# A graph-convolution stage on one core: eight of 32 edge rows fetched by GpSimd's indirect DMAs instead of selected by one-hot matmuls

## The chip, the cores and the metric

The kernel runs on one NeuronCore of a Trainium2 chip. The metric is device time in microseconds of the whole program, from one launch; the lower the better. The engines are called PE (TensorE, the matmuls; PEld is its weight load), DVE (VectorE), ACT (ScalarE), POOL (GpSimd) and SP (SyncE, which here only issues DMAs).

## The reference

Two networks run on one graph of 12,500 nodes and 412,500 edges (400,000 drawn at random plus a loop at every node; `src` and `dst` are inputs and come sorted by `dst`). The first is a two-layer graph convolution with 16 features in, 32 hidden, 16 out:

```
deg  = segment_sum(ew with loops of weight 1, dst)
dis  = where(deg > 0, rsqrt(deg), 0);  norm = dis[src] * ew * dis[dst]
h    = relu(segment_sum((x  @ W1.T)[src] * norm, dst) + b1)
out  =      segment_sum((h  @ W2.T)[src] * norm, dst) + b2
x    = layernorm(x + out)        # over the 16 features
```

The second is a mesh network on the result: an edge encoder, a node encoder, and two rounds of edge MLP, segment sum over `dst` and node MLP, with a decoder. Its output is added to x, and a last layer norm over the features follows. The change concerns the graph convolution alone, and there the two lines with `segment_sum(... [src] ...)`: for each edge, a row of a table of 12,500 x 16 floats is taken by `src`, weighted, and added up by `dst`.

## The kernel before, in words

**Sorting.** The edges lie in 128 rows (one for each partition), each of 3,328 slots (`RL`), and each row spans a short stretch of destinations. A bitonic network on DVE sorts every row by source; the key is source times 128 plus the destination's offset from the row's base, and the edge weight moves along. The sorted keys are then taken apart: the source modulo 256 goes to DRAM as bf16 (`mod_d`), the source's block of 256 relative to a planned first block (`slot_t`), the destination's offset (`drel_t`) and the weight (`ew_t`) are turned by TensorE, so that 128 edges lie on the partitions. A row is then 26 tiles (`NS`) of 128 edges.

**Messages.** `messages(table, fill)` is called twice, once for each convolution. It fills the table, writes it to DRAM, and splits it into three bf16 parts that sum to the float (`parts3`, into `t3`, which stays in SBUF: 256 sources on two halves of 128 partitions, blocks of 256 along the free axis). A hardware loop of four trips then takes 32 rows (`RI`) a trip, with the loop's body written out. For each row:

- `load` (L577) has SP fetch the row's 3,328 values of `mod_d` broadcast to 128 partitions, 832 KB; this is issued one row ahead.
- `half_row` (L583) makes the one-hot over the source modulo 256, in bf16, two DVE operations of 128x1664 for each half of the row. `begin` (L589, L591) makes `wm`, which picks the block and carries the edge weight.
- `select` takes the row's 26 tiles in six packs, of 4, 4, 5, 5, 4 and 4 tiles. For each tile, six bf16 matmuls (L607: three parts by two halves of 128 sources) gather up to seven candidate blocks of 16 features per edge into PSUM. DVE makes the destination one-hot `ohd` (L611) and multiplies PSUM by `wm` into `msg` (L614).
- `add_up` (L623) multiplies `msg` by `ohd` on TensorE in fp32, one matmul for each tile (two instructions in the records), one pack behind `select`. After the last pack ACT copies the row's sum out of PSUM (L629).
- `fold_up` (L635, L639) adds the seven blocks with one matmul, and DVE adds the result to `agg` at the row's base.

The tile framework sets the order of each engine's instructions in this stage by its own planning; SP and POOL have queues of their own. POOL has nothing to do here. In the later edge stages it issues the indirect DMAs of `gather` (L415), each of which fetches 128 rows of 64 floats by 128 indices.

Names used below: L385 is the one-hot of the edge stage on DVE (two SBUF inputs, fp32, 128x512), L1116 another (one bf16 input), L405 the addition to a window, L1175 the edge update; L566 and L570 are the copies at the start of each trip of the message loop.

Of the kernel before, what the change touches and what calls it, by code (L numbers as in the profile page):

```python
# [9 lines left out]
F32 = mybir.dt.float32  # L10
I32 = mybir.dt.int32
BF16 = mybir.dt.bfloat16
# [19 lines left out]
RI = 32  # L32
EPS = 1e-5
# [4 lines left out]
def gcn_then_mesh_gnn_kernel(ctx: ExitStack, tc: tile.TileContext, a: dict, out: bass.AP):  # L38
# [86 lines left out]
    def bank(name):  # L125
        return psum.tile([128, 512], F32, name=f"ps_{name}")
# [80 lines left out]
    slot_t = so.tile([P, NS, NR], F32, name="slot_t")  # L207
    drel_t = so.tile([P, NS, NR], F32, name="drel_t")
    ew_t = so.tile([P, NS, NR], F32, name="ew_t")
    with tc.tile_pool(name="sort", bufs=1) as sp, \  # L210
# [94 lines left out]

        mod = sp.tile([NR, RL], BF16, name="mod")
# [35 lines left out]
        for t, to in ((free, slot_t), (k, drel_t), (vals[turn], ew_t)):  # L342
            for j0 in range(0, NS, 4):
                n = min(4, NS - j0)
                pt = pp.tile([128, 512], F32, name="ps_st", bufs=2)
                for j in range(n):
                    nc.tensor.transpose(pt[:, j * NR:(j + 1) * NR], tiles(t)[:, j0 + j, :], ident)
                nc.scalar.copy(to[:, j0:j0 + n, :], pt[:, :n * NR].rearrange("e (j r) -> e j r", r=NR))
# [156 lines left out]
    with tc.tile_pool(name="gcn", bufs=1) as gp, tc.tile_pool(name="gcnw", bufs=2) as gw:  # L505
# [10 lines left out]
        ior = gp.tile([P, LR], F32, name="ior")  # L516
        nc.gpsimd.iota(ior, pattern=[[1, LR]], base=0, channel_multiplier=0, allow_small_or_imprecise_dtypes=True)
# [34 lines left out]
        def messages(table, fill):  # L552
# [10 lines left out]
            with tc.tile_pool(name="rows", bufs=2) as rw:  # L563
                with tc.For_i(0, trip_count(2, NR // RI)) as it:
# [7 lines left out]
                    slot, drel, ew = mine  # L572
                    rows, loaded, sums, folds = {}, {}, [], []

                    def load(r):
                        loaded[r] = rw.tile([128, RL], BF16, name="mod")
                        nc.sync.dma_start(loaded[r], mod_d[ds(it * RI + r, 1), :].to_broadcast([128, RL]))  # L577

                    def half_row(r, h):

                        oh = rw.tile([128, 2, RL // 2], BF16, name="roh", bufs=3)
                        for i in range(2):
                            nc.vector.tensor_scalar(oh[:, i, :], loaded[r][:, h * (RL // 2):(h + 1) * (RL // 2)],  # L583
                                                    iof[:, i:i + 1], None, op0=OP.is_equal)
                        return oh

                    def begin(r):
                        wm = rw.tile([P, NS, SB], F32, name="wm")
                        nc.vector.tensor_tensor(wm, iow[:, None, :SB].to_broadcast([P, NS, SB]),  # L589
                                                slot[:, :, r:r + 1].to_broadcast([P, NS, SB]), op=OP.is_equal)  # L590
                        nc.vector.tensor_tensor(wm, wm, ew[:, :, r:r + 1].to_broadcast([P, NS, SB]), op=OP.mult)  # L591
                        ohs = [None, None]
                        h = packs[0][0] // (NS // 2)
                        ohs[h] = half_row(r, h)
                        rows[r] = ohs, wm, bank("seg")

                    def select(r, j0, n, sb):
                        ohs, wm, acc = rows[r]
                        pg = bank("h")
                        for j in range(j0, j0 + n):  # L600
                            h, at = divmod(j, NS // 2)
                            if ohs[h] is None:
                                ohs[h] = half_row(r, h)
                            b = first_block[r, j] * F
                            for i in range(3):
                                for u in range(2):
                                    nc.tensor.matmul(pg[:, (j - j0) * sb * F:(j - j0 + 1) * sb * F],  # L607
                                                     ohs[h][:, u, at * P:(at + 1) * P], t3[:, i, u, b:b + sb * F],
                                                     start=(i == u == 0), stop=(i == 2 and u == 1))
                        ohd = rw.tile([P, 5, LR], F32, name="ohd", bufs=3)  # L610
                        nc.vector.tensor_tensor(ohd[:, :n, :], ior[:, None, :].to_broadcast([P, n, LR]),  # L611
                                                drel[:, j0:j0 + n, r:r + 1].to_broadcast([P, n, LR]), op=OP.is_equal)
# [28 lines left out]
                    load(0)  # L641
                    for r in range(RI):
                        if r + 1 < RI:
                            load(r + 1)
                        begin(r)
                        for i, pack in enumerate(packs):
                            sums.append(select(r, *pack))
                            if len(sums) > 1:
                                add_up(*sums.pop(0))
                            if folds and i >= 2:  # L650
                                fold_up(*folds.pop(0))
                    add_up(*sums.pop(0))
                    fold_up(*folds.pop(0))
# [659 lines left out]
```

## Time and profile before

| | us |
|---|---|
| median of three runs | 15415.33 (15409.99 to 15437.33) |
| the profiled execution | 15403.32 |
| its span, first to last instruction | 15401.6 |
| busy PE / DVE / POOL / ACT over the span | 11359.6 / 8752.5 / 6386.7 / 2374.3 |

The profile records one execution; 1.7 us of it lie outside the span. In the order of time: the sort until about 800 us, the degrees until about 1300 us, the first message loop until about 3005 us, the second, after the layer between, from about 3130 to 4840 us, and the two edge stages up to the end. The message loops run at a clock of 0.99 of full speed, with PE busy 98% of the time, and POOL is idle in them. A row of the profile names the line, the engine, the operation, output and inputs, and shape; a bracket at its end tells how long the engine was idle before it and what released it.

### The profile page before, as it was taken

The page shows a single profiled execution, that of the slowest core. Times are in us where ns is not written, and L with a number is a line of the kernel's source. Part 1 is how long each engine was busy: PE and PEld are TensorE (multiplying, and loading weights), DVE is VectorE, ACT ScalarE, POOL GpSimd, SP SyncE. Part 2 cuts the span into 40 slices and gives each one's busy share as a digit, 9 for nine tenths or more (in the row PEclk, how much of TensorE's full clock was granted, in tenths as well). Part 3 has the DMA queues.
Part 4 walks back from the last instruction along what each step waited for, and adds up shares of the span by engine and source line. Part 5 has one row for each costly group of instructions (what it writes and reads, how often), then busy time and mean ns, then how long its engine had stood idle before and what let it go on. Part 6 is the DMA issues. An engine that isn't in the chain of part 4 may idle for free. (4 is left out here: it accounts for less than half of the span.)

```text
span 15401.6 us, 272960 instructions
## 1 busy us (share of the span) xinstructions
PE 11359.6 (74%) x104538; PEld 8563.0 (56%) x104539; DVE 8752.5 (57%) x22373; ACT 2374.3 (15%) x3731; POOL 6386.7 (41%) x6741
## 2 busy tenths in 40 slices
PE   0089999999998788888888888875666666666665
PEld 0078999889997455555555555553444444444443
DVE  9977777677777455455555555553444444444444
ACT  3400000000000222222222222221111111111111
POOL 0000000000001555556556665555666666666665
PEclk9999999999997688788888888886777777777777
DMA  0001111111111222222222222222222222222222
GB/s 29 0 15 54 66 64 66 50 67 66 65 65 47 56 59 59 58 60 62 59 59 62 59 62 60 60 60 59 61 60 60 61 60 60 61 60 60 61 59 50
DMA packets 958543, 871.49 MB, mean 57 GB/s; under 512 B 599416, under 2 KB 706192, under 8 KB 956548
## 3 DMA queue, kind: packets, MB, share of 16 engines
q1 hardware_dynamic: 258034, 493.54, 9.5%
q0 software_dynamic: 207360, 212.75, 6.8%
q10 hardware_dynamic: 491796, 147.08, 4.1%
q8 instruction: 859, 14.07, 0.4%
q14 instruction: 494, 4.05, 0.1%
HBM read 718.12 MB, written 134.51 MB: 55 GB/s over the span
## 5 line engine op out<-in xcount | busy, mean ns | idle before, releaser
L415 POOL DMA_INDIRECT pg<-tab_p,si x6480 | 6293.6, 971 | 3901.1 <-issue 1707.5
L1052 PE MATMUL ps_o<-eb_w,h 128*128 128x128 f32 x6480 | 1389.3, 381 | 1822.1 <-ACT h L1045 1623.5
L1052 PEld LDWEIGHTS ps_o<-eb_w,h 128*128 128x128 f32 x6480 | 1184.3, 274 | 2078.7 <-ACT h L1045 1762.4
L607 PE MATMUL ps_h<-t,roh 128*128 128x112 bf16 (+1 forms) x39936 | 2131.9, 211 | 65.9 <-DVE roh L583 65.9
L607 PEld LDWEIGHTS <-roh 128*128 128x128 bf16 x39936 | 2011.2, 98 | 115.3 <-issue 112.0
L789 POOL MEMSET zero<- 64x192 bf16 x1 | 0.3, 252 | 4015.1 <-DVE agg L639 4015.1
L1116 DVE TENSOR_SCALAR ot<-rb,iop 128x512 bf16<-128x512 bf16 x810 | 295.5, 365 | 2349.4 <-DMA rb<-relg_d 1482.8
L623 PE MATMUL ps_seg<-ohd,msg 128*112 128x112 f32 (+1 forms) x13312 | 1618.5, 266 | 0.0
L474 DVE TENSOR_REDUCE var<-sq 128x8 f32<-128x512 f32 (+2 forms) x1290 | 843.1, 666 | 1291.8 <-issue 743.9
L397 PE MATMUL ps_seg<-oh,y 128*64 128x64 f32 x19440 | 1298.7, 255 | 208.6 <-issue 197.9
L623 PEld LDWEIGHTS ps_seg<-ohd,msg 128*112 128x112 f32 (+1 forms) x13312 | 1407.4, 172 | 0.5
L397 PEld LDWEIGHTS ps_seg<-oh,y 128*64 128x64 f32 x19440 | 1141.8, 166 | 370.3 <-issue 348.0
L1040 PE MATMUL ps_h<-e,eb_w 128*128 128x512 f32 x1620 | 1193.3, 820 | 64.2 <-issue 36.4
L614 DVE TENSOR_TENSOR msg<-ps_h,wm 128x448 f32<-128x448 f32 (+1 forms) x1536 | 975.0, 635 | 460.5 <-PE ps_h L607 455.0
L611 DVE TENSOR_TENSOR ohd<-ior,rdrel 128x448 f32<-128x448 f32 (+1 forms) x1536 | 1011.1, 659 | 235.3 <-PE ps_seg L623 235.3
L473 ACT ACTIVATE sq<-ps_o 128x512 f32<-128x512 f32 (+1 forms) x1240 | 735.4, 593 | 2587.6 <-remote 668.8
L1045 ACT ACTIVATE h<-ps_h,eb_b 128x512 f32<-128x512 f32 x810 | 556.7, 687 | 3047.7 <-remote 2019.4
L1040 PE MATMUL ps_h<-ot,qd 128*128 128x512 bf16 x2430 | 784.4, 424 | 110.1 <-issue 97.3
L479 DVE TENSOR_TENSOR y<-ps_o,rs_y 128x512 f32<-128x512 f32 x1215 | 802.8, 688 | 88.1 <-issue 4.6
L385 DVE TENSOR_TENSOR oh<-iow,drl 128x512 f32<-128x512 f32 x1215 | 830.0, 683 | 14.4 <-DMA drl<-rel_d 7.2
L1042 PE MATMUL ps_h<-ident,pg 128*128 128x128 f32 x3240 | 603.1, 296 | 309.9 <-issue 236.5
L1052 PE MATMUL ps_o<-ee_w,h 128*128 128x128 f32 x3240 | 626.6, 353 | 238.5 <-ACT h L1033 232.8
(280 smaller groups left out, 11483.2 us busy)
## 6 DMA issues: line engine op xcount, KB each, us to landing
mod<-mod_d SPq DMA_DIRECT2D x256, 832.0 KB
pg<-tab_p,si POOLq DMA_INDIRECT x6480
e_d<-e SPq DMA_DIRECT2D x405, 256.0 KB
e<-e_d SPq DMA_DIRECT2D x405, 256.0 KB
rb<-relg_d ACTq DMA_DIRECT2D x1612, 64.0 KB
qd<-tab_q ACTq DMA_DIRECT2D x1612, 24.0 KB
at<-in_attrT SPq DMA_DIRECT2D x405, 32.0 KB
tab_q<-tabs SPq DMA_DIRECT2D x50, 187.5 KB
```

What stands on the lines that cost most here:

```text
L385: nc.vector.tensor_tensor(oh, iow[:, None, :].to_broadcast([P, K, W]), drl[:, g * K:(g + 1) * K, None].to_broadcast([P, K, W]), op=OP.is_e ...
L397: nc.tensor.matmul(ps[r:r + n, :W], v, oh[:, k, :], start=(k == 0), stop=(k == K - 1))
L415: nc.gpsimd.indirect_dma_start(out=to[:, k, :], out_offset=None, in_=table, in_offset=bass.IndirectOffsetOnAxis(ap=idx[:, k:k + 1], axis=0))
L473: nc.scalar.activation(sq, o.rearrange("p (k f) -> p k f", f=D), AF.Square, scale=D ** -0.5)
L474: nc.vector.tensor_reduce(v[:, i:i + k], sq, axis=AX.X, op=OP.add)
L479: nc.vector.tensor_tensor(y, o, r[:, i:i + k, None].to_broadcast(list(y.shape)), op=OP.mult)
L607: nc.tensor.matmul(pg[:, (j - j0) * sb * F:(j - j0 + 1) * sb * F], ohs[h][:, u, at * P:(at + 1) * P], t3[:, i, u, b:b + sb * F], start=(i ...
L611: nc.vector.tensor_tensor(ohd[:, :n, :], ior[:, None, :].to_broadcast([P, n, LR]), drel[:, j0:j0 + n, r:r + 1].to_broadcast([P, n, LR]), o ...
L614: nc.vector.tensor_tensor(msg[:, :n * sb * F].rearrange("p (j s f) -> p j s f", s=sb, f=F), pg[:, :n * sb * F].rearrange("p (j s f) -> p j ...
L623: nc.tensor.matmul(acc[:sb * F, :LR], msg[:, j * sb * F:(j + 1) * sb * F], ohd[:, j, :], start=(j0 + j == packs[0][0]), stop=((j0, n, sb) ...
L1040: nc.tensor.matmul(ph, w, v, start=(i == 0), stop=False)
L1052: nc.tensor.matmul(po[:, j * 128:(j + 1) * 128], h[:, j * P:(j + 1) * P], w1, start=False, stop=(j == KP - 1))
```

## The change

Eight of a trip's 32 rows (3, 6, ... 24) no longer go through `load`, `half_row`, `select`, `add_up` and `fold_up`. For them:

- After the sort, the full source numbers are also turned by TensorE, and the eight rows' part of each trip is kept as int32 (`src_t`). To make room, `slot_t` and `drel_t` become bf16.
- `fetch(i)` has POOL issue 26 indirect DMAs, each of which fetches 128 table rows of 16 floats from DRAM, into one of three buffers `xg`. Two fetches are issued at the start of a trip, and the others as earlier ones are begun.
- `gathered(i)` works on DVE and PE in ten pieces, one after each pack of the ordinary rows: multiply `xg` by the weight; split it into three bf16 parts (`parts3`, five operations); six times make a bf16 one-hot over 128 destinations for up to five tiles, with the 26 matmuls (one-hot as weights, 48 moving columns) one piece behind; copy the sum out on ACT; turn and add the three parts with three fp32 matmuls, and add to `agg`.
- `due` starts a gathered row with the ordinary rows number 4, 6, 9, 11, 13, 16, 18 and 20 of the 24.

The ordinary rows are begun one row ahead, their `begin` now in six steps, one after each pack (both halves' one-hots, and `wm`), and `load` is issued two rows ahead. `ohd` is issued ahead of the pack's matmuls rather than after them. PE, DVE and ACT are issued in the order of the source (`manual_schedule`), not in a planned one.

```diff
-    slot_t = so.tile([P, NS, NR], F32, name="slot_t")
-    drel_t = so.tile([P, NS, NR], F32, name="drel_t")
+    slot_t = so.tile([P, NS, NR], BF16, name="slot_t")
+    drel_t = so.tile([P, NS, NR], BF16, name="drel_t")
+    src_t = so.tile([P, NS, NR // RI * len(GR)], I32, name="src_t")
...
+        nc.vector.tensor_single_scalar(kj, ki, 7, op=OP.arith_shift_right)
+        nc.vector.tensor_copy(vals[1 - turn], kj)
+        srcf = sp.tile([P, NS, NR // RI, len(GR)], F32, name="srcf")
+        turned_tiles(vals[1 - turn], lambda j0, n, v: nc.scalar.copy(
+            srcf[:, j0:j0 + n], v.rearrange("e j (i r) -> e j i r", r=RI)[:, :, :, GR.start:GR.stop:GR.step]))
+        nc.vector.tensor_copy(src_t, srcf.rearrange("e j i r -> e j (i r)"))
...
                     def begin(r):
-                        wm = rw.tile([P, NS, SB], F32, name="wm")
...
+                        loaded_r = loaded.pop(r)
                         ohs = [None, None]
...
+                        first = packs[0][0] // (NS // 2)
+                        for h in (first, 1 - first):
+                            ohs[h] = rw.tile([128, 2, RL // 2], BF16, name="roh", bufs=3)
+                            for i in range(2):
+                                nc.vector.tensor_scalar(ohs[h][:, i, :], loaded_r[:, h * (RL // 2):(h + 1) * (RL // 2)],
+                                                        iof[:, i:i + 1], None, op0=OP.is_equal)
+                                yield
+                            if h == first:
...
                     def select(r, j0, n, sb):
+                        ohd = rw.tile([P, 5, LR], F32, name="ohd", bufs=3)
+                        nc.vector.tensor_tensor(ohd[:, :n, :], ior[:, None, :LR].to_broadcast([P, n, LR]),
+                                                drel[:, j0:j0 + n, r:r + 1].to_broadcast([P, n, LR]), op=OP.is_equal)
...
+                    def fetch(i):
+                        xg = rw.tile([P, NS, F], F32, name="xg", bufs=3)
+                        for j in range(NS):
+                            nc.gpsimd.indirect_dma_start(
+                                out=xg[:, j, :], out_offset=None, in_=table,
+                                in_offset=bass.IndirectOffsetOnAxis(ap=srci[:, j, i:i + 1], axis=0))
+                        return xg
+
+                    def gathered(i, xg):
+                        r = GR[i]
+                        x3 = rw.tile([P, NS, 3, F], BF16, name="x3")
+                        acc = bank("o")
+                        def weigh_row():
+                            nc.vector.tensor_tensor(xg, xg, ew[:, :, r:r + 1].to_broadcast([P, NS, F]), op=OP.mult)
+                        def split():
+                            parts3(rw, "x3", xg, [x3[:, :, k, :] for k in range(3)])
+                        def some(j0):
+                            n = min(5, NS - j0)
+                            oh = rw.tile([P, 5, P], BF16, name="goh")
+                            nc.vector.tensor_tensor(oh[:, :n, :], ior[:, None, :].to_broadcast([P, n, P]),
+                                                    drel[:, j0:j0 + n, r:r + 1].to_broadcast([P, n, P]), op=OP.is_equal)
+                            return lambda: [nc.tensor.matmul(
+                                acc[:, :3 * F], oh[:, j, :], x3[:, j0 + j].rearrange("p k f -> p (k f)"),
+                                start=(j0 + j == 0), stop=(j0 + j == NS - 1)) for j in range(n)]
+                        def end():
+                            sl = rw.tile([P, 3 * F], F32, name="gsl")
+                            nc.scalar.copy(sl, acc[:, :3 * F])
+                            return sl
+                        def turn(sl):
+                            tot = bank("t")
+                            for k in range(3):
+                                nc.tensor.matmul(tot[:F, :P], sl[:, k * F:(k + 1) * F], ident, start=(k == 0), stop=(k == 2))
...
+                            nc.vector.tensor_add(w, w, tot[:F, :LR])
...
+                    others = [r for r in range(RI) if r not in GR]
+                    due = {-(-(234 * i + 340) // 100): i for i in range(len(GR))}
+                    fetched = {i: fetch(i) for i in range(2)}
...
+                        for m, r in enumerate(others):
+                            if m + 2 < len(others):
+                                load(others[m + 2])
+                            if m in due:
+                                i = due[m]
+                                pieces.append(gathered(i, fetched.pop(i)))
+                                if i + 2 < len(GR):
+                                    fetched[i + 2] = fetch(i + 2)
+                            beginning = begin(others[m + 1]) if m + 1 < len(others) else iter(())
+                            for i, pack in enumerate(packs):
+                                sums.append(select(r, *pack))
+                                if len(sums) > 1:
+                                    add_up(*sums.pop(0))
+                                if folds and i >= 2:
+                                    fold_up(*folds.pop(0))
+                                next(beginning, 0)
+                                piece()
...
+                    with tc.manual_schedule(engines={ET.PE, ET.DVE, ET.Activation}):
+                        in_order()
```

## The prediction

> **What bounds the kernel now.** I read the stretches of 500 us first, then groups and waits of the message loops, then their order in time, and last the gathers of the edge stage, since the change brings such gathers here.
>
> ```profile
> core 0: us, PE busy (x) PEld busy (x) DVE busy (x) ACT busy (x) POOL busy (x), PEclk, DMA share, GB/s
> 2000.00:2500.00 500.00, 492.23 (x7904) 480.99 (x7904) 394.10 (x720) 9.60 (x38) 0.00 (x0) 0.99 0.18 67
> ```
>
> PE is 98% busy at full clock, its weight loads too; DVE is at 79%, POOL idle.
>
> ```profile
> L607 PE MATMUL ps_h<-t,roh 128*128 128x112 bf16 (+1 forms) x39936 | 2131.9, 211 | 65.9 <-DVE roh L583 65.9
> L623 PE MATMUL ps_seg<-ohd,msg 128*112 128x112 f32 (+1 forms) x13312 | 1618.5, 266 | 0.0
> L614 DVE TENSOR_TENSOR msg<-ps_h,wm 128x448 f32<-128x448 f32 (+1 forms) x1536 | 975.0, 635 | 460.5 <-PE ps_h L607 455.0
> L611 DVE TENSOR_TENSOR ohd<-ior,rdrel 128x448 f32<-128x448 f32 (+1 forms) x1536 | 1011.1, 659 | 235.3 <-PE ps_seg L623 235.3
> ```
>
> In the idle columns DVE waits for PE; PE's 65.9 us fall at the trips' starts. The message loops are bound by PE.
>
> ```profile
> 1697.78 0.25 ACT L629 COPY sl<-ps_seg 112x112 f32<-112x112 f32 x1 [12.76 <-PE ps_seg L623]
> 1710.79 0.25 ACT L629 COPY sl<-ps_seg 112x112 f32<-112x112 f32 x1 [12.75 <-PE ps_seg L623]
> ...
> 2000.73 1.27 PEld L607 LDWEIGHTS <-roh 128*128 128x128 bf16 x24
> ...
> 2001.96 1.01 PEld L623 LDWEIGHTS ps_seg<-ohd,msg 128*96 128x96 f32 x10
> ...
> 2002.91 1.27 PEld L607 LDWEIGHTS <-roh 128*128 128x128 bf16 x24
> ```
>
> A row is 13.006 us. 24 selecting matmuls take 1.23 us (51 ns each), ten summing ones 0.95. The copies at a trip's start (L566) stand at 1299.0 and 1725.6: a trip is 426.6 us, of which 32 rows are 416.2; 5.1 lie ahead of the first matmul and 5.3 behind the rows. There are eight trips.
>
> **What goes.** Eight rows a trip: 8 x 13.0 = 104 us of PE.
>
> **What comes on PE.** Of 26 matmuls with 48 columns no row shows one. The L607 form with 96 columns goes at 44 ns (30 in 1.33 us), so 22 ns if only columns count; the weight load's own 98 ns is the other end. I take 45: 1.2 us. Three fp32 products of 128 columns are six records at some 107 ns (L623: 96 with 112 columns): 0.65. Together 1.85 us a gathered row, between 1.2 and 3.2.
>
> **What comes on DVE.** Weighing, 416 elements: 0.58 us (between L589, 208 in 0.369, and L611, 448 in 0.619). The split: two subtractions at 0.62 with the step between them, three casts between 0.41 (L371 casts 784 in 0.57) and the same 0.62: 2.5 to 3.1, taken 2.8. One-hots: 640 elements by L611's slope 0.82, less 0.085 of overlap with the next, five times, and a small one: 3.9. The addition: 0.26. In all 7.5 us. An ordinary row keeps 394.10/500 x 13.0 = 10.25 us. A trip on DVE is 24 x 10.25 + 8 x 7.5 = 306 us, below what follows for PE: it stays second.
>
> **The written order.** Between the end of a pack's selecting matmuls and the sum that needs its `msg`, PE has 0.8 + 1.23 = 2.03 us of other work; `msg` needs 0.25 to start and 0.62. DVE may thus run 1.1 us late before PE stops. A plain pack leaves DVE 2.75/6 = 0.46 us, so ordinary rows lose nothing. The one-hots of a gathered row (0.74, against 0.22 more on PE and the 0.46) just keep pace, but the split puts 2.8 us into one pack: 2.3 late, PE stops 1.2, and with what follows some 2 us a gathered row; from 0 to 4. `ohd` ahead of the matmuls costs nothing: the same wait of `msg` for PE comes behind it.
>
> If nothing else intervened, a trip were 10.4 + 24 x 13.006 + 8 x (1.85 + 2) = 353 us.
>
> **What comes on POOL.** 26 x 8 gathers a trip, 1664 in all. A gather has 128 descriptors, as in the edge stage; rows of 64 bytes rather than 256 should not change POOL's part.
>
> ```profile
> L415 POOL DMA_INDIRECT pg<-tab_p,si x6480: 942/947/1787, 5125.8 to 15311.7; - x197
> ...
> 12999.71 0.69 DVE L385 TENSOR_TENSOR oh<-iow,drl 128x512 f32<-128x512 f32 x1
> 13000.07 1.15 POOL L415 DMA_INDIRECT pg<-tab_p,si  x1 [0.30 <-issue]
> ...
> 13002.78 0.94 POOL L415 DMA_INDIRECT pg<-tab_p,si  x1 [0.30 <-issue]
> 13004.02 0.95 POOL L415 DMA_INDIRECT pg<-tab_p,si  x1 [0.30 <-issue]
> ...
> 9076.80 0.69 DVE L385 TENSOR_TENSOR oh<-iow,drl 128x512 f32<-128x512 f32 x1
> 9076.89 1.41 POOL L415 DMA_INDIRECT pg<-tab_p,si  x1 [0.30 <-issue]
> 9077.40 0.35 DVE L1116 TENSOR_SCALAR ot<-rb,iop 128x512 bf16<-128x512 bf16 x1
> ```
>
> Undisturbed, one follows another after 1.25 us (13002.78, 13004.02): 0.95 and 0.30 of issue. That is 32.5 us a row, not 25. And a gather that comes up while DVE runs an operation with two SBUF inputs is held until that one ends: at 13000.07 by (13000.40 - 13000.07) - 0.13 = 0.20 us, at 9076.89 by 0.46.
>
> Here the page "SBUF — State Buffer" of the Trainium skill (section "SBUF: two separate sides") speaks against the change: DVE and GpSimd share one pair of ports, whoever comes first has it for its whole instruction, and the other stands still. That holds for DVE operations in a two-port mode or with two SBUF inputs, so for `roh`, `ohd` and `wm`, twelve in a row. By the rule DVE would find a gather running 0.95/1.25 = 76% of the time, with 0.47 us left: 4.3 us more on an ordinary row and some 4 on a gathered one, DVE 24 x 14.5 + 8 x 11.5 + 10.4 = 450 us a trip, slower by 24 x 8 + 5 = 197 us (15,612). The trace confirms only the half about POOL: L385 takes 673 ns in the degree stage without gathers and 684 to 692 beside them. I take the trace: DVE loses next to nothing, POOL is held.
>
> How much: a gather meets an operation of length d (less 0.13) in proportion to it and then waits half of it. In 13.0 us there are four of 0.64 (`roh`), four of 0.62 and two of 0.74 (`ohd`), two of 0.37 (`wm`): the sum of half squares is 1.46, so 0.11 us a gather; a gathered row's own operations add 0.04. That is chance alone; operations in a regular beat can hit more. Taken 0.19 (0.08 to 0.35): 1.44 us from gather to gather.
>
> With copies first, the eighth row is in SBUF at 2.5 + 208 x 1.44 + 2 = 304 us of the trip (landing: above 0, below the 5.2 us of an 832 KB load at 1299.0; taken 2). DVE wants it in ordinary row 20, at 5.1 + 20 x 13.006 + 7 x 3.85 = 292. So POOL is late by 12 us, spread over the last gathered rows; since DVE runs in order, everything behind the weighing waits, then PE. Behind it come four rows (52.0), the last gathered one (3.9), the tail (5.3), and 2 us because PE after a pause is slow (46 matmuls in 4.24 us at 1304.65, 92 ns each): 367 us.
>
> **Small things.** The sort's chain gains two operations of 1.9 us and a copy: 5 us once; 26 transposes hide beside DVE's. `load` two rows ahead waits on SP for the buffer as before (L577 waits for `roh`) and has 13 us where a trip's first needs 5.2 (1299.0 to 1304.1): nothing; without that lead DVE would wait 5 us a row. DMA: q0's share of 6.8% of 16 engines over 829,440 fetched rows is 20 ns each; 212,992 rows are 266 us of all 16, in loops at 0.18: nothing.
>
> **Sum.** (426.6 - 367.2) x 8 = 475 us less 5: 15,403 becomes 14,933. The profiled execution is 12 us under the median of the runs shown, so 14,945.
>
> **Rivals.**
>
> *PE sets the pace (28%).* Gathers arrive in time, if a gather takes 1.38 us or less: 353 us a trip, (73.2 x 8) - 5 = 581 us gained, 14,834. For it: the `due` rows leave each gathered row 30 us plus its own work. Without stalls of the written order it is 14,710 or so.
>
> *Gathers decide against it (13%).* One mechanism: DVE's operations follow each other without a gap (`roh`, one-hot, `ohd`), and the gather is let in only at the end of such a run. Runs of 1.2 us, and 1.8 with a one-hot, give by the same half squares 0.6 us a gather: 1.85, the eighth row at 389 us, a trip of 452, in all 207 + 5 slower: 15,627. It decides from 1.72 us a gather on, where 2.5 + 208 x 1.72 + 2 + 63.2 reaches 426. For it: three gathers of 1.69 to 1.79 us, held over L1175, L405 and L385 in turn. Against: at 9076.89 L1116 follows L385 without a gap, and the gather was let go at L385's end.
>
> *The whole-instruction lock* above, 2%. That the gathers come to nothing is excluded: the PE work of eight rows is gone by construction.
>
> **Chances.** POOL paces mildly: 55%, its own range 14,850 to 15,150. PE paces: 28%. No change, by a gather near 1.72: about 4%. Slower: 13% together. A measurement of this kernel can tell some 0.2% (31 us) from no change. The range 14,760 to 15,400 leaves out the slower cases and the least stalled PE case.
>
> **What would show it.** L629's copies 13.0 us apart in ordinary rows, about 15 to 17 around gathered ones; trips of 367 us; 8144 indirect gathers, those of the message loops with a mean near 1.14 us; DVE's weighing waiting for the gathers' DMA late in a trip, hardly early; `ohd` within 3% of 619 ns. Wrong: no wait at the weighing (PE paces), waits from the third row on and gathers above 1.4 us (slower), `roh` or `ohd` longer by tenths (the lock), or PE waiting for `msg` in ordinary rows (the order).

## The result, and the profile after

The change made the kernel slower: 16221.19 us (median of 16209.02 to 16231.08) against 15426.33 (15409.99 to 15458.08), a ratio of 1.0518 with a 95% interval of 1.0490 to 1.0545. The profiled execution took 16225.74 us. The forecast was 14,945 us, within 14,760 to 15,400.

One thing must be known to read what follows. The runs fell on several chips, and they differ in one respect. In these first runs and on chip 7 the kernel before takes 15,390 to 15,426 us; on chips 1, 5, 12, 14 and 15 it takes 13,427 to 13,439. I call the first **A** and the others **B**; a row of a table compares only runs of one chip.

| | before, us | after, us | ratio (95%) |
|---|---|---|---|
| A, first runs | 15426.33 | 16221.19 | 1.0518 (1.0490 to 1.0545) |
| A, chip 7 | 15389.79 | 16219.56 | 1.0533 (1.0496 to 1.0571) |
| B, chip 5 | 13431.36 | 13189.97 | 0.9820 (0.9803 to 0.9836) |

So the same change costs 5% on A and gains 1.8% on B. First the profile after on A. The same 500 us in the message loop, where PE had been busy for 492:

```profile
core 0: us, PE busy (x) PEld busy (x) DVE busy (x) ACT busy (x) POOL busy (x), PEclk, DMA share, GB/s
2000.00:2500.00 500.00, 341.98 (x4760) 305.52 (x4757) 270.84 (x516) 6.90 (x29) 235.02 (x208) 0.80 0.13 41
```

POOL now works, and PE and DVE both work less. The groups that answer to those shown of before (L628 is the selecting matmul, L641 the summing one, L632 `msg`, L620 `ohd`; the columns are busy time and mean, then idle time before and what ended it):

```profile
L628 PE MATMUL ps_h<-t,roh 128*128 128x112 bf16 (+1 forms) x29952 | 1807.0, 217 | 906.1 <-issue 839.8
L641 PE MATMUL ps_seg<-ohd,msg 128*112 128x112 f32 (+1 forms) x9984 | 1369.4, 277 | 377.6 <-issue 357.6
L632 DVE TENSOR_TENSOR msg<-ps_h,wm 128x448 f32<-128x448 f32 (+1 forms) x1152 | 724.3, 629 | 1790.1 <-remote 1251.6
L620 DVE TENSOR_TENSOR ohd<-ior,rdrel 128x448 f32<-128x448 f32 (+1 forms) x1152 | 750.6, 652 | 0.0
```

The instructions themselves are no longer than before (`ohd` 652 ns, 659 before). New is the idle time: L628 had waited 65.9 us in all, now 906.1, and nearly all of it is "issue", which means that PE waits for nothing that the profile shows. `msg` waits 1251.6 us for "remote", a signal whose sender the profile doesn't name.

ACT's copies of the rows' sums (L647) tell where these waits fall; the trip is the second, which starts at 1851.6:

```profile
1973.20 0.25 ACT L647 COPY sl<-ps_seg 112x112 f32<-112x112 f32 x1 [124.21 <-PE ps_seg L641]
1986.21 0.25 ACT L647 COPY sl<-ps_seg 112x112 f32<-112x112 f32 x1 [12.75 <-PE ps_seg L641]
...
2026.54 0.25 ACT L647 COPY sl<-ps_seg 112x112 f32<-112x112 f32 x1 [14.01 <-PE ps_seg L641]
...
2058.42 0.25 ACT L647 COPY sl<-ps_seg 112x112 f32<-112x112 f32 x1 [26.48 <-PE ps_seg L641]
```

The first row comes out 122 us after the trip's start; on B it needs 22. Then rows stand 13.0 to 15.2 us apart, much as forecast, except for five, which take 32 (2058.42 - 2026.54). A trip is 540 us. Without gathers it is 348 (e1 below, on B); some 99 more fall at the start, and the remaining 93 in and beside the five. What happens at the start:

```profile
1351.54 0.95 POOL L663 DMA_INDIRECT xg<-tab,rsrc  x1 [0.30 <-issue]
1352.69 0.10 PEld L628 LDWEIGHTS <-roh 128*128 128x128 bf16 x1 [2.69 <-issue]
1352.80 0.96 POOL L663 DMA_INDIRECT xg<-tab,rsrc  x1 [0.31 <-issue]
1354.06 0.95 POOL L663 DMA_INDIRECT xg<-tab,rsrc  x1 [0.30 <-issue]
1354.09 0.24 PE L628 MATMUL ps_h<-t,roh 128*128 128x96 bf16 x1 [2.56 <-issue]
...
1356.89 0.24 PE L628 MATMUL ps_h<-t,roh 128*128 128x96 bf16 x1 [2.56 <-issue]
```

A weight load, 1.40 us, a matmul, 1.40 us: PE issues one instruction in 1.40 us, in the middle of a pack whose operands are all there. Meanwhile POOL's gathers follow each other every 1.26 us. Three buffers `xg` stand open, so 78 gathers run until 100 us into the trip; the five rows of 32 us are those beside which the 26 gathers of one more row run. The stretch with gathers, and one after the last of them:

```profile
1320.00:1415.00 95.00, 14.33 (x83) 8.16 (x82) 4.86 (x9) 0.00 (x0) 69.86 (x73) 0.54 0.08 14
1425.00:1440.00 15.00, 15.00 (x232) 14.71 (x231) 10.96 (x21) 0.25 (x1) 0.00 (x0) 0.96 0.16 59
```

(Columns as in the stretches above.) 83 matmuls in 95 us with 73 gathers, 232 in 15 us without any. DMA is at 8%, so this isn't a full DMA. The clock of 0.54 doesn't explain it either: before makes 46 matmuls in 4.42 us (1304.66) at a clock of 0.52, not one in 2.80 us. And PE stays slow after the last gather:

```profile
1410.86 0.96 POOL L663 DMA_INDIRECT xg<-tab,rsrc  x1 [0.30 <-issue]
...
1415.69 0.24 PE L628 MATMUL ps_h<-t,roh 128*128 128x96 bf16 x1 [2.56 <-issue]
...
1422.69 1.28 PE L641 MATMUL ps_seg<-ohd,msg 128*96 128x112 f32 x6 [0.90 <-issue]
```

In all eight trips it is back at its pace only 10.7 to 12.2 us after the last of the 78 gathers begins, though that gather's transfers end 2.7 us after it begins. The same stretch of the same kernel on B:

```profile
1320.00:1415.00 95.00, 94.10 (x1516) 90.46 (x1515) 82.32 (x155) 1.97 (x8) 76.27 (x62) 1.00 0.24 71
```

62 gathers, and PE is 99% busy. Now the rows of 32 us, and a wait for "remote": near 1505, in the first trip, DVE waits for `msg`'s matmuls.

```profile
1495.03 1.34 PE L628 MATMUL ps_h<-t,roh 128*128 128x112 bf16 x24
...
1505.76 0.62 DVE L632 TENSOR_TENSOR msg<-ps_h,wm 128x448 f32<-128x448 f32 x1 [8.95 <-remote]
...
1516.51 0.62 DVE L632 TENSOR_TENSOR msg<-ps_h,wm 128x448 f32<-128x448 f32 x1 [9.04 <-remote]
```

The 24 matmuls end at 1496.4, and DVE goes on 9.4 us later. From 1492 to 1513 POOL gathered without a break, one every 1.26 us. I read it as a loop: a gather that comes up under DVE's operations is held (it then takes up to 2.06 us, shown below), so a working DVE slows POOL down; when PE falls behind, DVE pauses, the gathers flow at 1.26 us, and PE falls farther behind. Counting matmuls and weight loads that PE started in each 5 us, from 1300 to 2900 us, against the gathers begun in the 10 us around its start (by itself such a count doesn't tell which is the cause):

| gathers in 10 us | 4 | 5 | 6 | 7 | 8 |
|---|---|---|---|---|---|
| after, A | 145.6 | 136.1 | 75.8 | 46.8 | 15.7 |
| after, B | 155.4 | 151.7 | 146.2 | 141.6 | 94.6 |

(B's last column mixes 22 stretches of 133 to 174 starts with 19 of 0 to 89, among them those where DVE waits for a gathered row. The most that A has there is 79.)

The profile of before already showed it, in the edge stage. The forecast quotes gathers there at 13000.07 to 13004.02; they run on to 13012, and this is ACT, and PE's matmuls for `ps_o`, in the same 12 us:

```profile
13002.46 0.69 ACT L1045 ACTIVATE h<-ps_h,eb_b 128x512 f32<-128x512 f32 x1 [6.96 <-remote]
13003.20 2.08 PE L1052 MATMUL ps_o<-eb_w,h 128*128 128x128 f32 x8 [4.22 <-ACT h L1045]
...
13012.40 0.60 ACT L473 ACTIVATE sq<-ps_o 128x512 f32<-128x512 f32 x1 [9.25 <-remote]
```

PE's matmuls end at 13005.28, and ACT goes on at 13012.40, 7.1 us later, in the last gather of the burst. That is also where A and B differ in the kernel before. For B these are its stages in the traces of c6 and e3 below. Up to the first edge gather A and B agree to a microsecond (trips of 426.6 us on A and 426.5 on B, the first edge gather at 5125.8 and 5125.4); then the first edge step takes 13.1 us for each group of eight gathers on A and 10.1 on B, the second 11.9 and 10.1.

### The profile page after: what moved, and what is told of

The parts are those of the page before. It is cut to its first block, busy times and chain, and to the rows that moved or that the text cites. A ratio compares the mean times of both kernels' runs of the same rounds, so it can differ in the third digit from the quotient of the medians.

```text
span 16223.8 us, 250465 instructions
## 1 busy us (share of the span) xinstructions
PE 10994.0 (68%) x93172; PEld 8052.3 (50%) x93173; DVE 8473.5 (52%) x22000; ACT 2372.5 (15%) x3738; POOL 8328.2 (51%) x8405
## 5 line engine op out<-in xcount | busy, mean ns | idle before, releaser
L663 POOL DMA_INDIRECT xg<-tab,rsrc x1664 | 1880.5, 1130 | 2911.7 <-DVE rsrc L589 1559.5
L1159 PE MATMUL ps_o<-eb_w,h 128*128 128x128 f32 x6480 | 1422.8, 388 | 1841.6 <-ACT h L1152 1684.9
L628 PE MATMUL ps_h<-t,roh 128*128 128x112 bf16 (+1 forms) x29952 | 1807.0, 217 | 906.1 <-issue 839.8
L628 PEld LDWEIGHTS <-roh 128*128 128x128 bf16 x29952 | 1587.3, 101 | 1039.0 <-issue 1032.9
L632 DVE TENSOR_TENSOR msg<-ps_h,wm 128x448 f32<-128x448 f32 (+1 forms) x1152 | 724.3, 629 | 1790.1 <-remote 1251.6
L641 PE MATMUL ps_seg<-ohd,msg 128*112 128x112 f32 (+1 forms) x9984 | 1369.4, 277 | 377.6 <-issue 357.6
L641 PEld LDWEIGHTS ps_seg<-ohd,msg 128*112 128x112 f32 (+1 forms) x9984 | 1156.5, 181 | 452.4 <-issue 432.7
L1147 PE MATMUL ps_h<-e,eb_w 128*128 128x512 f32 x1620 | 1157.1, 799 | 45.6 <-DMA qd<-tab_q 23.5
L1159 PEld LDWEIGHTS ps_o<-ee_w,h 128*128 128x128 f32 x3240 | 534.1, 250 | 508.7 <-ACT h L1140 461.0
```

The costliest lines, as they stand in the source:

```text
L632: nc.vector.tensor_tensor(msg[:, :n * sb * F].rearrange("p (j s f) -> p j s f", s=sb, f=F), pg[:, :n * sb * F].rearrange("p (j s f) -> p j ...
L641: nc.tensor.matmul(acc[:sb * F, :LR], msg[:, j * sb * F:(j + 1) * sb * F], ohd[:, j, :], start=(j0 + j == packs[0][0]), stop=((j0, n, sb) ...
L663: nc.gpsimd.indirect_dma_start(out=xg[:, j, :], out_offset=None, in_=table, in_offset=bass.IndirectOffsetOnAxis(ap=srci[:, j, i:i + 1], ax ...
L1147: nc.tensor.matmul(ph, w, v, start=(i == 0), stop=False)
L1159: nc.tensor.matmul(po[:, j * 128:(j + 1) * 128], h[:, j * P:(j + 1) * P], w1, start=False, stop=(j == KP - 1))
```

## Experiments

My theory (1): gathers that follow each other freely starve PE's issue and hold back its signals. Rivals: (2) the written order of PE, DVE and ACT is at fault; (3) the port: gathers and DVE hold each other, and POOL paces.

**The gathers replaced by one plain transfer a row (e1).**

```diff
-                        for j in range(NS):
-                            nc.gpsimd.indirect_dma_start(out=xg[:, j, :], ...)
+                        nc.sync.dma_start(xg, table[:P * NS, :].rearrange("(p j) f -> p j f", j=NS))
```

> The kernel after, with each gathered row's 26 indirect gathers replaced by one plain DMA of SP that brings 3328 consecutive rows of the table into the same buffer (the rows fetched are not those of the edges' sources; all other work is left as it is). Theory 1 (gathers that follow each other freely starve TensorE's issue and hold back its signals): a trip falls from 540 us to 353-360, the program to 14,770-14,850 us. Theory 3 (a shared port: gathers and VectorE's operations hold each other, so POOL paces): the same, as there is no gather. Theory 2 (the written order of TensorE, VectorE and ACT is at fault): the pause of 124 us at the start of a trip and the rows of 32 us stay, the program above 15,400 us.

**The order alone (e2)**: all 32 rows ordinary.

```diff
-                    others = [r for r in range(RI) if r not in GR]
-                    due = {-(-(234 * i + 340) // 100): i for i in range(len(GR))}
-                    fetched = {i: fetch(i) for i in range(2)}
+                    others = list(range(RI))
+                    due = {}
+                    fetched = {}
```

> The kernel after with all 32 rows as ordinary rows in the written order and no row gathered. By my prediction's steps (an ordinary row costs 13.0 us in the written order): a trip of about 426 us and about 15,430 us, as before. Theory 2 (the order costs it): a trip well over 450 us, in the direction of 16,200 us. Theories 1 and 3: as by my steps.

**The gathers alone (e3)**: in before, at the head of each trip:

```diff
+                    for i in range(8):
+                        xg = rw.tile([P, NS, F], F32, name="xg", bufs=3)
+                        for j in range(NS):
+                            nc.gpsimd.indirect_dma_start(out=xg[:, j, :], ..., ap=some_rows[:, j:j + 1], ...)
```

> The kernel before, its planned order untouched, with POOL issuing 208 gathers in each trip into a buffer that nothing reads (index values made by an iota). So the only thing added beside the message rows is the gathers. Theory 1: TensorE is starved while they flow; POOL needs 260 us for them if nothing holds them, and with TensorE at a third of its pace or less in that time the trip grows from 427 us to 500-600, the program to 16,000-16,800 us. Theory 2: no change, 15,430 us. Theory 3: VectorE's operations hold the gathers, but nobody waits for these, so no change beyond what VectorE loses; under 15,500 us.

**26 plain transfers a row (e7)**, each of 128 pieces of 64 bytes:

```diff
-                            nc.gpsimd.indirect_dma_start(out=xg[:, j, :], ...)
+                            nc.sync.dma_start(xg[:, j, :], table[j * P:(j + 1) * P, :])
```

> The kernel after, with each of the 26 gathers of a row replaced by a plain DMA of SP for 128 consecutive rows of the table (so not the rows of the edges' sources): as many transfers of as many pieces of the same size as the gathers, but no descriptor written by POOL. It splits theory 1. If the transfers themselves starve TensorE, the trip stays near 540 us and the program near 16,200; if it is POOL's writing of descriptors, the trip falls to 353-370 and the program to 14,770-14,900 us.

These met B (before: 13,426.69 us). e1: 12,815.16 us, a trip of 348.2 us. e2: 13,434.38, a trip of 426.5. e3: 13,434.45, a trip of 426.7. e7: 12,986.27, a trip of 370 (each of these is one run). My theory failed for this chip: gathers beside the planned rows cost PE nothing, though they came 1.44 us apart (1,664 gathers in 1880.9 us of work and 508.6 of gaps). The 500 us of e3, from its trace on chip 5, are those of before with POOL at work:

```profile
2000.00:2500.00 500.00, 492.03 (x7907) 480.50 (x7905) 393.92 (x718) 9.33 (x37) 256.77 (x228) 0.99 0.23 71
```

So did theory 2: the written order costs 0 us a trip on B. e1 gives what the change is worth without its gathers: (426.5 - 348.2) x 8 = 626 us of trips, 611.5 of the program.

**The kernel after again**, to see it and before on one chip; **six rows, doled (c5)**; **a filler behind each gather (e4)**.

> The kernel after as it is. In the four runs just made the kernel before took 13,427 us, not 15,426, and gathers added to it (e3) cost nothing, so what starved TensorE in the first runs is not always there. Where the kernel before takes about 13,430 us: without starvation the trip should come out near the 353-370 us of my steps, like the kernels without gathers (348 and 369 us), and the program at 12,830-13,000 us, faster than before by 3-4%. If the written order or the gathers' being held by VectorE (theories 2 and 3) are at fault, it stays slower than before: above 13,430 us. Where the kernel before takes about 15,420 us: 16,220 us again.

c5: DVE copies the indices of one slot (two after a row's last pack) after each pack, and only those gathers can follow.

```diff
-GR = range(3, 27, 3)
+GR = range(4, 28, 4)
...
+                            ix = rw.tile([P, 2], I32, name="ix", bufs=4)
+                            nc.vector.tensor_copy(ix[:, :n], srci[:, j:j + n, i])
+                            for k in range(n):
+                                nc.gpsimd.indirect_dma_start(out=xg[:, j + k, :], ..., ap=ix[:, k:k + 1], ...)
...
-                    due = {-(-(234 * i + 340) // 100): i for i in range(len(GR))}
+                    due = {m: i for i, m in enumerate((5, 9, 13, 16, 20, 24))}
...
+                                fetch_some(2 if i == 5 else 1)
```

> Six rows of 32 gathered instead of eight, and their gathers doled out: VectorE copies the indices of one or two slots after each pack, and only those gathers can follow, seven to an ordinary row, so gathers stop when VectorE stops and flow no faster than one in about 1.9 us. By my steps a trip is 26 x 13.0 + 6 x 1.85 + some 20 = about 370 us. Theory 1 with starvation present (before at 15,420): no pause at the trip's start, no rows of 32 us, a trip of 370-400 us, the program 14,950-15,200, faster than both kernels. With starvation absent (before at 13,430): 12,950-13,100 us, a little slower than the kernel after. Theory 2: slower than before in both.

e4:

```diff
                             nc.gpsimd.indirect_dma_start(out=xg[:, j, :], ...)
+                            nc.gpsimd.memset(pad, 0.0)
+                            nc.gpsimd.memset(pad, 0.0)
```

> The kernel after with two POOL memsets of 128x256 (about 0.3 us each) behind every gather of the message rows, so that gathers follow each other at 1.9 us instead of 1.25 where nothing holds them. Theory 1 with starvation present: though POOL has more to do, the trip shortens from 540 us to 420-480. With starvation absent: POOL's 208 x 1.9 = 395 us a trip become the pace, 400-430 us, the program 13,250-13,500 us. Theory 3: POOL paces either way, the trip is longer than the kernel after has in the same conditions.

These met A, on chip 7 (before: 15,389.79 us). After: 16,219.56, trips of 540 us. c5: 14,982.94, ratio to before 0.9735 (0.9695 to 0.9774), trips of 383.5 us. e4: 15,865.90 (one run), trips of 498, where theory 1 expected 420 to 480.

e4 isn't the even spacing I wanted. POOL's order is planned, and the planner put only one memset between gathers, the others in bunches, behind which gathered rows are late (up to 47 us for a row; DVE waits 301.6 us for gathers in all). But at the trip's start, before any row is late, it tells what I asked:

```profile
1330.62 0.96 POOL L664 DMA_INDIRECT xg<-tab,rsrc  x1 [0.16 <-issue]
1331.58 0.33 POOL L667 MEMSET pad<- 128x256 f32 x1
1332.07 0.96 POOL L664 DMA_INDIRECT xg<-tab,rsrc  x1 [0.16 <-issue]
...
1341.11 1.21 POOL L664 DMA_INDIRECT xg<-tab,rsrc  x1 [0.16 <-issue]
1342.32 0.34 POOL L668 MEMSET pad<- 128x256 f32 x1
1342.82 1.22 POOL L664 DMA_INDIRECT xg<-tab,rsrc  x1 [0.16 <-issue]
...
1320.00:1415.00 95.00, 81.98 (x1104) 72.39 (x1102) 60.91 (x110) 1.30 (x6) 85.61 (x116) 0.93 0.17 52
```

A gather that nothing holds now follows the one before after 1.45 us instead of 1.26, and the mean over the stretch is 1.65. PE makes 1,104 matmuls in those 95 us instead of 83 (89 in the kernel after on this chip), and the first row of a trip comes out after 22 to 35 us, not 122. POOL did more, and PE was freed: theory 3 can't have that, nor theory 2, for the order is the same. c5 in the same 95 us:

```profile
1320.00:1415.00 95.00, 91.36 (x1457) 87.36 (x1454) 76.36 (x182) 1.71 (x7) 53.61 (x47) 1.00 0.19 60
```

47 gathers, 1,457 matmuls, no pause, no row above 16.3 us. But plain rows mostly stand 13.6 to 13.7 us apart where c5 on B, below, has 13.0, and a trip is 16 us longer than there, so the price is not all gone. And some 100 us of c5's gain lie in the edge stages, which it doesn't touch (10,174 us from their first gather, against 10,276 in before); why isn't known.

**Once more, to part A from B.** The runs so far left A without e1, e3 and e7. First these again, and a memset behind each gather of the first edge step of before (c6):

> The kernel before with 208 gathers a trip that nothing reads, once more, now that two conditions are known: one in which the kernel before takes 13,427 us and gathers cost TensorE nothing, one in which it takes about 15,400 us. Where before takes about 15,400 us, theory 1 expects the trip to grow from 427 us to 500-600 and the program to 16,000-16,800 us; theories 2 and 3 expect no change. Where before takes about 13,430 us: 13,434 us again.

> The kernel after with one plain DMA of SP in place of each row's 26 gathers (the rows fetched are not those of the edges' sources), once more. Where before takes about 15,400 us, theory 1 expects the trip of 348 us that it had where before took 13,427, as no gather runs beside the rows, and 14,750-14,850 us in all; theory 2 the pause at the trip's start and a program above 15,400 us.

> The kernel after with 26 plain DMAs of SP in place of a row's 26 gathers (again not the rows of the edges' sources), once more. Where before takes about 15,400 us: if it is POOL's writing of descriptors that starves TensorE, the trip of 369 us stays and the program takes 14,900-15,000 us; if it is the many small transfers, the trip goes to 450 us or more and the program to 15,600-16,300 us.

```diff
                 in_offset=bass.IndirectOffsetOnAxis(ap=idx[:, k:k + 1], axis=0))
+            if pad is not None:
+                nc.gpsimd.memset(pad, 0.0)
```

> The kernel before with one POOL memset of 128x256 (about 0.3 us) behind each gather of the first edge step, so that its eight gathers a group take 12.5 us instead of 10. There a group takes 13.0 us where the kernel before takes about 15,400 us. Theory 1: gathers farther apart starve TensorE less, the group falls to 12.6-12.8 us and the program by 80-160 us. If gathers 1.56 us apart starve it as much as gathers 1.25 us apart do, TensorE is short of its pace for longer and the group grows to 14 us or more, the program by 400 us or more. Where before takes 13,427 us POOL paces that step and the program grows by about 3240 x 0.31 = 1000 us.

All met B (before: 13,436.26): 13,442.17, 12,809.12, 12,986.71, and c6 14,635.01. c6 says nothing on spacing, as the planner bunched its memsets too (ten at 6002.95, after eight gathers 1.25 us apart). It shows that POOL alone paces the first edge step on B: a group goes from 10.1 to 13.1 us on average, for eight memsets (2.5 us).

Then the change itself, c5, e3 and e1:

> The kernel after as it is, once more, for the condition that it has not met yet. Where before takes 13,430 us: by my steps a trip of 353-370 us; from e1 and e7 (348 and 369 us a trip without gathers) and from e3 (gathers 1.44 us apart beside the rows) 12,815-13,000 us, 3-4.5% faster than before. Where before takes about 15,400: 16,220 us.

> The kernel with six gathered rows and its gathers doled out, once more, for the other condition. Where before takes 13,430 us: a trip of 371-384 us, 13,000-13,100 us, faster than before by 2.5-3% but behind the kernel after by some 1%. Where before takes about 15,400: 14,980 us.

> The kernel before with 208 gathers a trip that nothing reads. Where before takes about 15,400 us: theory 1 expects a trip of 500-600 us instead of 427 and a program of 16,000-16,800 us; theories 2 and 3 no change. Where before takes 13,430: 13,440 us.

> The kernel after with one plain DMA in place of each row's 26 gathers (the rows fetched are not those of the edges' sources). Where before takes about 15,400 us: theory 1 expects a trip of 348 us and 14,750-14,850 us in all, theory 2 above 15,400 us. Where before takes 13,430: 12,812 us.

B again, on chip 5 (before: 13,431.36): after 13,189.97, ratio 0.9820 (0.9803 to 0.9836); c5 13,046.89, ratio 0.9708 (0.9692 to 0.9724); e3 13,436.70; e1 12,816.84. Here the change does what it was forecast to do, less well than I then expected (12,815 to 13,000), and c5, expected 1% behind it, is 1.1% ahead. The change's trip is 387.5 us, where e1 on the same chip has 348.2. The weighing (L676) tells the difference, first on A, then on B:

```profile
L676 DVE TENSOR_TENSOR xg<-xg,rew x64: 583/584/589, 1470.7 to 5697.1; 128x416 f32<-128x416 f32 x64
...
L676 DVE TENSOR_TENSOR xg<-xg,rew x64: 582/589/594, 1371.6 to 4471.7; 128x416 f32<-128x416 f32 x64
its engine sat idle before it (us, times) until:
  DMA xg<-tab,rsrc: 317.8, 32
```

On B DVE waits 317.8 us for gathers, 39.7 a trip, which is the difference between the trips (39.3). On A it never does: POOL is always ahead of the slow PE. Why POOL is late on B, two stretches of its timeline show, from a trip's start and from the middle of one:

```profile
1320.14 0.96 POOL L663 DMA_INDIRECT xg<-tab,rsrc  x1 [0.30 <-issue]
1321.41 0.96 POOL L663 DMA_INDIRECT xg<-tab,rsrc  x1 [0.31 <-issue]
...
2303.82 2.06 POOL L663 DMA_INDIRECT xg<-tab,rsrc  x1 [0.30 <-issue]
2306.19 2.06 POOL L663 DMA_INDIRECT xg<-tab,rsrc  x1 [0.30 <-issue]
```

And what DVE does in the second:

```profile
2303.32 0.81 DVE L684 TENSOR_TENSOR goh<-ior,rdrel 128x640 bf16<-128x640 f32 x1
2304.06 0.60 DVE L620 TENSOR_TENSOR ohd<-ior,rdrel 128x448 f32<-128x448 f32 x1
2304.59 0.60 DVE L632 TENSOR_TENSOR msg<-ps_h,wm 128x448 f32<-128x448 f32 x1
2305.13 0.63 DVE L606 TENSOR_SCALAR roh<-mod,iof 128x1664 bf16<-128x1664 bf16 x1
2305.68 0.81 DVE L684 TENSOR_TENSOR goh<-ior,rdrel 128x640 bf16<-128x640 f32 x1
```

The gather of 2303.82 ends at 2305.88. It came up under L684, which ended at 2304.13, and L620 followed without a gap until 2304.66. Had it been let in at L684's end, as at 9076.89 in before, it would have been done with 0.81 us more, at 2304.94. It was held through L620 at least, and what of the further 0.4 us falls on `msg` and `roh` the records don't tell. In such packs one gather gets through for each: rival two's mechanism. It meets 264 of the 1,664 gathers (over 2.0 us each), which hold some 300 of the 510 us that all of them take beyond 0.95 each. Over a trip the gathers come (327.5 - 2.9)/207 = 1.57 us apart.

Again e3 and e1, for A:

> The kernel before, its planned order untouched, with 208 gathers a trip that nothing reads. Where before takes about 15,400 us: theory 1 expects gathers alone to starve TensorE, a trip of 500-600 us instead of 427 and a program of 16,000-16,800 us; less if VectorE's planned order holds the gathers more than 1.5 us apart, as the doled ones are in the six-row kernel (383 us a trip against 367 where before takes 13,430): then about 440-450 us a trip and 15,520-15,600. Theories 2 and 3: no change. Where before takes 13,430: 13,440 us.

> The kernel after with one plain DMA in place of each row's 26 gathers (the rows fetched are not those of the edges' sources). Where before takes about 15,400 us: theory 1 expects a trip of 348 us and 14,750-14,850 us in all, theory 2 above 15,400 us. Where before takes 13,430: 12,812 us.

B (before: 13,439.07): 13,437.41 and 12,819.47. And six rows without the doling (c8), after with the two lines `GR` and `due` of c5:

> Six gathered rows at the same places in the order as in the doled kernel, but their gathers left free as in the kernel after (two rows fetched ahead at the trip's start, the next whenever a buffer comes free). It parts the doling from the number of rows. Where before takes 13,430 us: POOL needs 156 x 1.58 = 247 us of 367, so no gathered row is late; a trip of 366-370 us, 13,010-13,060 us, as the doled kernel: the gain over the kernel after there is POOL's load alone. Where before takes about 15,400 us: theory 1 expects the pause of about 100 us at the trip's start again and some rows of 30 us, a trip of 450-520 us, the program 15,550-16,100 us, while the doled kernel takes 383 and 14,983.

B (before: 13,430.99): 13,037.73, ratio 0.9706 (0.9690 to 0.9722), trips of 365 us, no wait of L676 at all. So on B the gain of c5 over the change is POOL's smaller load, and the doling brings nothing.

**What stays open.** That the gathers alone starve PE on A, beside an order that is planned, was not run on A; e3 met B each time. That PE's pace there hangs on the gathers' spacing is shown on one order (after and e4 on chip 7), and not what stands between them: whether POOL's issuing or the transfers, e7 would have told on A. Both are over some 8 us before PE is back at its pace, so something is still queued then, and the records don't name it. On A it isn't parted how much of c5's gain is the doling and how much the smaller number of gathers. And what makes A differ from B isn't known; it may be the chip or the time of the run.

One rival stands untested: the recording itself. A DMA sends 16 landing signals, and the traces of A lack most of their records just where A is slow. Before on A has all 608 for the 38 DMAs issued from 2000 to 2500 us, where it agrees with B, but 44,177 of 177,312 in the edge stages; c6, on B, has 172,855 of these. In the 95 us from 1320, after has 175 of 1,152 on A, e4 562 of 1,008, and after on B 1,076 of 1,104. The instructions' own records are not short there (all 29,952 of L628 are in the trace of after on A), so it is the signals' that are lost. No wait in a trace of B is put down to "remote". Every execution here was recorded, as each has a span and a clock, so it may be the recording of the gathers' signals, and not the gathers, that PE waits behind on A; the gathers' spacing changes both alike.

On A c5 is the best version here, 2.65% faster than before, where the change is slower. On B it is 2.92% faster, and c8 as much (2.94%).

## Why the prediction was wrong

**Wrong on A: the step that costs nothing.** The sum takes what the gathers do to DVE, to POOL and to the share of DMA, and lets PE run at 13.0 us a row beside them. Nothing in it prices PE's issue or its signals; "Small things" puts the gathers' transfers at nothing because DMA has room, and room it had (8%). That missing term is 192 us a trip of 540: 99 in the pause and 93 in five rows. What on A makes PE wait, the gathers or their recording, stays open. Bounds from both sides were set on POOL and DVE only. The row that could have told was in the stage that I read for the gathers' 1.25 us: ACT idle for 9.25 us, in the same 12 us, and groups of eight gathers that took 11.9 us where POOL needed 10.0. I took POOL's rows there and not who else stood still.

**The rivals.** The slower rival (15,627, from 1.72 us a gather on) ended on the right side for a wrong reason: in it POOL is late and DVE waits for gathers. On A no weighing waited. That the direction came out as in its 13% is luck.

**Right on both: the rest of the sum.** The written order costs no more than taken: the trip of e1 is 348.2 us, so a gathered row costs (348.2 - 10.4 - 24 x 13.006)/8 = 3.2 us of PE and stalls, where 1.85 + 2 = 3.85 was taken. Rows of e1 stand 13.0 us apart, or 14.1 to 14.8 beside gathered work. `ohd` has a median of 619 ns with gathers beside it: DVE loses next to nothing, and the whole-instruction lock holds for POOL nearly alone, as read from the trace. Nearly: 37 of the change's 768 `roh` on B are over 8% longer, and in six of e3's eight trips (chip 5) the fp32 copy of `rew` takes some 819 ns beside a gather, 586 in before. The sort's added work came to 11.6 us (L566 at 1299.0, L581 at 1310.6), where 5 was taken.

**Right in mechanism, mis-sized on B: 1.44 us a gather.** "POOL paces mildly", trip 367 us, is what happened there, with 388. In before's order the spacing is 1.44 (e3). In the written order it is 1.57, as beside the `goh` a gather is held over a run of operations; the half-square estimate let it wait for one operation by chance. With 1.57 in its own line, the eighth row is there at 2.5 + 208 x 1.57 + 2 = 331 us; measured, it is weighed 327 to 332 us into the trip. The trip of 387.5 would be (426.5 - 387.5) x 8 - 5 = 307 us gained; 241 were, since the edge stages, which the change doesn't touch, took 64 us more on the same chip (8,371 us from their first gather, against 8,307 in e3), 62 of them in 6,480 gathers that are 9 to 10 ns longer each (966 and 957 ns). On A they took 93 us less than in before (10,183 and 10,276). Why isn't known.

**Sure of too much.** Faster with 83% was a chance over terms that had been bounded. POOL is idle in the message loops of before, so no row there shows PE beside a gather, and that term stood at nothing without a bound.

## What to carry to other kernels

Where work is brought to an engine that was idle in a stage, look in a stage where that engine already does it at all the others, not at its own rows alone: idle times that end with "remote" or "issue" when its burst ends may be its price. Give such work a pace: let it depend on the engine that it could starve (a small copy of its indices in that engine's order), so that it stops when that one stops; that cost 9 us of 13,038 where it wasn't needed (c5 and c8 on B, two chips). And repeat a comparison on another chip before a mechanism is believed: here the sign of the change hangs on it. Compare also how complete the two traces are.

## What the runs showed of the hardware that I had not expected

- On A, beside indirect gathers at 1.26 us from one to the next PE starts one instruction in 1.40 us, and DVE and ACT go on 7 to 9 us after its matmuls end; with gathers 1.45 us apart at the least and 1.65 on average PE is 86% busy in the same stretch. PE's slowness outlasts the last gather by some 11 us. On B eight gathers in 10 us stand beside up to 174 starts of PE in 5 us. Whether A would do so unrecorded isn't known.
- The same program takes 15,390 us on one chip and 13,431 on another. Stages without gathers agree to a microsecond; the two edge steps, whose gathers run from end to end, take 29 and 18% longer on A, and there its trace holds a quarter of the landing signals' records, B's 97%.
- A gather that comes up in a gapless run of DVE operations takes 2.06 us, where one undisturbed takes 0.95; DVE's `ohd` beside it keeps its 619 ns, while an fp32 copy took 819 ns beside a gather instead of 586.
